# A two-layer attention and expert kernel: a third buffer, earlier clears, and VectorE work given to ScalarE and GpSimd

## The chip, the core and the metric

The kernel runs on one core of a Trainium2 chip. A core has five engines with queues of their own: TensorE (PE; PEld is its weight load) multiplies matrices, VectorE (DVE) works on elements, ScalarE (ACT) applies functions, GpSimd (POOL) works on elements and issues indirect DMAs, and SyncE (SP) issues the other DMAs. Each engine takes its instructions in the order in which they stand in its queue, and semaphores hold an instruction until what it needs is there. The metric is device time in microseconds, the median of several runs.

## The reference

The input x has 8 batches of 112 rows and 256 columns, the context 8 batches of 375 rows and 256 columns. All is in float32. `_layernorm` normalises over the columns, with 1e-5 added to the variance.

```python
x = x + xattn0(layernorm(x), ctx)          # 16 heads of 16, biases, softmax over 375 keys
x = x + moe(layernorm(x))                  # 8 experts, 2 per row, hidden 1024, exact gelu
x = x + xattn1(layernorm(x), ctx, mask)    # no biases; softmax((q k + mask) / 16)
x = x + bitffn(layernorm(x))               # ternary weights, depthwise conv over 3 rows, silu
```

In `moe`, a row is projected into a ball (x Wp + bp, scaled to a norm of at most 0.95), its hyperbolic distance to 8 centroids gives the logits, the two nearest experts are taken, and their outputs are weighted by a softmax of the two. In `bitffn`, both weight matrices (w1 is 1024 x 256, w2 is 256 x 1024) are first made ternary: `s = 1 / clip(mean(abs(w)), 1e-5)`, `clip(round(w * s), -1, 1) / s`.

## The kernel before

**Stages.** Layer 0's attention runs from 0 to about 302 us of the profiled span, with the router of the expert layer woven into it; the experts run to about 465, layer 1's attention to about 681, the ternary feed-forward part to the end.

**One attention batch.** The 16 heads are four groups of four, and the four heads of a group sit at partitions 0, 32, 64 and 96 of TensorE. For batch b the steps are: `norm` (the layer norm is applied, L224 to L226, and n is turned to nT), `query` (t_q, then qd = scaled t_q on VectorE, L560 in layer 0 and L564 in layer 1, then eight DMAs that spread the heads over the partitions, `apart`), `key` (t_k, kd on ScalarE, eight or more DMAs by `apart`), `value` (t_v, copied to v by VectorE, L589 or L593), and for each group g `scores` (sc, and the negated maximum of each row into top, L605 in layer 0; with the mask, L612, in layer 1), once `lower` (the maxima are turned and added to q, giving qa, L625), for each group `turned` (t_p = keys times qa, so that the softmax's exponent comes out with keys on partitions; in layer 1 VectorE adds the mask in four pieces of 336 elements, L645; ScalarE takes Exp into pT, L647) and `weighted` (po = pT times v, L657), and then `finish_o`, `finish_t` and `project` (division by the sum, turn, output product, addition to x at L691 and the next norm's statistics).

**Order.** Both layers run through a plan (L699 to L767), a list of (slot, place, step) that is sorted by slot and place, four slots for each batch. With n = 4b: norm at n-5, key n-4, query n-3, value n-2, scores n+g, lower n+4, turned n+5+g, weighted n+6+g, finish_o n+10, finish_t n+11, project n+12. In layer 0, routing steps 0 to 7 of batch b come at slots n+13 to n+20: step 0 is `Router.norm` (rn, L291 to L294), step 6 is `place` (L371 to L393), which scatters the rows rn to the two places of the row in the DRAM array tok, by two indirect DMAs of GpSimd (L386). The plan of layer 0 has also: `clear` (L187 to L191), which writes zeros over one eighth of tok (slots 4 to 11) or ysc (slots 14 to 21), 0.9 MB each, by DMAs of SP; and the steps that make the weights ternary (L449 to L476, slots 8 to 19): for each of two weights of 2048 elements a partition, two sums of absolute values on VectorE (L457), a product with ones, a small sum and a reciprocal (L465 on), and three element steps. The order on SP is that of the plan; on the other engines a scheduler orders the instructions by their dependences and estimated costs, with the plan as priority.

**Layer norm.** `ln_stats` (L213 to L222) takes mean and variance on VectorE (L216, L218), adds 1e-5 (L219), and calls `rsqrt` (L193 to L211): two integer operations make a first guess, and three Newton steps refine it; for one column that is nine instructions on VectorE, all of one element a partition. The kernel has 32 such norms.

**Layer 1's start.** `combine` (L516 to L528) gathers each row's two expert outputs from ysc with indirect DMAs of GpSimd (L523), and adds them to x on VectorE (L527).

**Buffers.** The pool `ap` has 2 buffers for each name, `ap3` 3, `ap6` 6. rn comes from `ap`. The PSUM pairs are three, shared by t_k, t_v, sc and t_p. The small products of the router and the ternary sums share a bank with po.

```python
for slot, place, step, args in sorted(plan, key=lambda s: s[:2]):
    step(*args)
```

Of the kernel before, what the change touches and what calls it, by code (L numbers as in the profile page):

```python
# [12 lines left out]
F32 = mybir.dt.float32  # L13
# [3 lines left out]
ALU = mybir.AluOpType  # L17
# [37 lines left out]
def xattn_ffn_kernel(  # L55
# [17 lines left out]
    def const(shape, name, dt=F32):  # L73
        return cp.tile(shape, dt, tag=name, name=name)
# [89 lines left out]
    vbuf = [kp.tile([KC, NKC, H, 2 * A], F32, tag="v", name="v") for _ in range(3)]  # L164
    for v in vbuf:
        nc.gpsimd.memset(v, 1.0)
    desc = const([128, E], "desc")
    first = const([128, E], "first")
    for e in range(E):
# [43 lines left out]
    def ln_stats(b):  # L213

        st = sp.tile([S, 6], F32, tag="bnst", name="bnst")
        nc.vector.bn_stats(st, xs[b])  # L216
        mv = sp.tile([S, 2], F32, tag=f"mv{b}", name="mv")
        nc.vector.bn_aggr(mv, st)  # L218
        nc.vector.tensor_scalar_add(mv[:, 1:2], mv[:, 1:2], 1e-5)  # L219
        rs = sp.tile([S, 1], F32, tag=f"rs{b}", name="rs")  # L220
        rsqrt(mv[:, 1:2], rs, 1, "ln")
        return mv, rs  # L222

    def ln_apply(dst, b, stats):  # L224
        mv, rs = stats
        nc.vector.tensor_scalar(dst, xs[b], mv[:, 0:1], rs, ALU.subtract, ALU.mult)  # L226


    kv = [[None] * B, [None] * B]
# [27 lines left out]
    class Router:  # L257
# [30 lines left out]
            nc.vector.tensor_scalar_min(self.cn, self.cn, 0.99)  # L288
            nc.vector.tensor_scalar(self.cn1, self.cn, -1.0, 1.0, ALU.mult, ALU.add)

        def norm(self, b, stats):  # L291
            n = self.pool.tile([S, D], F32, tag="r_n", name="rn")
            ln_apply(n, b, stats)
            return n  # L294

# [152 lines left out]
    def ternary(small):  # L448

        steps = []  # L450
        for i in range(2):
            raw, half = raws[i], F * D // 256
            part, sc = const([128, 16], f"part{i}"), const([128, 1], f"sc{i}")

            def sums(i=i, raw=raw, part=part):
                for h in range(2):
                    yield lambda h=h: nc.vector.tensor_reduce(  # L457
                        part[:, 8 * h : 8 * h + 8],
                        raw[:, h * half : (h + 1) * half].rearrange("p (g n) -> p g n", g=8),
                        AX.X, ALU.add, apply_absolute_value=True,  # L460
                    )

            def scale(i=i, part=part, sc=sc):
                t = small("t_w")
                nc.tensor.matmul(t, ones, part, start=True, stop=True)  # L465
                nc.vector.tensor_reduce(tmean[i], t, AX.X, ALU.add)
# [3 lines left out]
            steps += [  # L470
                *sums(), scale,
                lambda raw=raw, sc=sc: nc.vector.tensor_scalar(raw, raw, sc, 1.0, ALU.mult, ALU.min),
                lambda raw=raw: nc.vector.tensor_scalar(raw, raw, -1.0, MAGIC, ALU.max, ALU.add),
                lambda i=i, raw=raw: nc.vector.tensor_scalar_sub(tern[i], raw, MAGIC),
            ]
        return steps  # L476
# [15 lines left out]
    def attention(layer, stats, stats_next):  # L492
        scale = (0.25, 0.0625)[layer]
        res = None
        with (
# [33 lines left out]

            def norm(b):  # L530
                n = ap.tile([S, D], F32, tag="n", name="n")
                ln_apply(n, b, stats.pop(b))
                if layer == 0:
                    nc.gpsimd.tensor_add(xs[b], xs[b], rowt[:S, D : 2 * D])
# [14 lines left out]
            def query(b):  # L549
                nT = st[b].pop("nT")  # L550
                t = misc("t_q")[:, : 2 * S].rearrange("p (o s) -> p o s", o=2)
                for o in range(2):
                    for c in range(2):
                        nc.tensor.matmul(  # L554
                            t[:, o, :], wts[layer]["q"][:, c, o * 128 : (o + 1) * 128], nT[:, c, :],
                            start=(c == 0), stop=(c == 1),
                        )
# [23 lines left out]
            def value(lay, b):  # L581
                v = kv[lay][b][1]
                t = pair("t_v").rearrange("p i n -> p (i n)")
                for i in range(NKC):
                    value_products(lay, b, i, t[:KC, i * D : (i + 1) * D])
                tv = t[:KC, : NKC * D].rearrange("p (i h a) -> p i h a", i=NKC, a=A)
                if lay == 0:
                    for i in range(NKC):
                        nc.vector.tensor_tensor(  # L589
                            v[:, i, :, 0:A], tv[:, i], rowt[:KC, 0:D].rearrange("p (h a) -> p h a", a=A), ALU.add  # L590
                        )
                else:
                    nc.vector.tensor_copy(v[:, :, :, 0:A], tv)  # L593

            def scores(b, g):

# [31 lines left out]
            def turned(b, g):  # L628
# [11 lines left out]
                for m in range(2):  # L640
                    pT = ap6.tile([KC, 2, NKC * S], F32, tag="pT", name="pT")
                    src = ts[m][:KC, :, : NKC * S]
                    if layer == 1:
                        for i in range(2):
                            nc.vector.tensor_tensor(pT[:, i, :], src[:, i, :], maskT_t, ALU.add)  # L645
                        src = pT
                    nc.scalar.activation(pT, src, AF.Exp)  # L647
                    pTs.append(pT)
# [48 lines left out]
            def add(slot, place, step, *args):  # L697
                plan.append((slot, place, step, args))
# [20 lines left out]
            if layer == 0:  # L719
# [335 lines left out]
```

## Time and profile before

| | |
|---|---|
| median of 3 runs | 786.43 us (785.28 to 789.81) |
| the profiled execution | 775.37 us, its span 773.7 us |
| TensorE busy | 624.8 us, 81% |
| VectorE busy | 462.2 us, 60% |
| ScalarE busy | 225.0 us, 29% |
| GpSimd busy | 48.9 us, 6% |
| mean granted TensorE clock | 0.832 |

The page cuts the span into 40 slices of 19.3 us; a digit is the busy share of a slice in tenths, and PEclk is the clock that TensorE was granted, in tenths.

```profile
PE   5778998969988953999999994999999988744143
DVE  6754769657665484011111105967998897589975
PEclk9787997878977875999999997559999998856557
DMA  3368468731201011697889943101111000000001
```

The experts are the block of nines in the PE row, with VectorE at 0 and 1. In the two attention stages both engines are high, and the clock falls where the PE row falls. The DMA row is high from the fourth to the eighth slice of layer 0, where the clears, the contexts and the first expert weights are loaded. The DMA issues that matter (count, KB each, median time from issue to landing):

```profile
tok<-zero SPq DMA_DIRECT2D x8, 896.0 KB, 5.2
ysc<-zero SPq DMA_DIRECT2D x8, 896.0 KB, 4.4
```

In a timeline a row is an instruction, or several of one kind, with start and length in microseconds; the brackets hold the idle time before it on its engine and the instruction that ended it.

### The profile page before, as it was taken

The page shows a single profiled execution, that of the slowest core. Times are in us where ns is not written, and L with a number is a line of the kernel's source. Part 1 is how long each engine was busy: PE and PEld are TensorE (multiplying, and loading weights), DVE is VectorE, ACT ScalarE, POOL GpSimd, SP SyncE. Part 2 cuts the span into 40 slices and gives each one's busy share as a digit, 9 for nine tenths or more (in the row PEclk, how much of TensorE's full clock was granted, in tenths as well). Part 3 has the DMA queues.
Part 4 walks back from the last instruction along what each step waited for, and adds up shares of the span by engine and source line. Part 5 has one row for each costly group of instructions (what it writes and reads, how often), then busy time and mean ns, then how long its engine had stood idle before and what let it go on. Part 6 is the DMA issues. An engine that isn't in the chain of part 4 may idle for free.

```text
span 773.7 us, 15030 instructions
## 1 busy us (share of the span) xinstructions
PE 624.8 (81%) x5650; PEld 450.1 (58%) x5650; DVE 462.2 (60%) x1663; ACT 225.0 (29%) x452; POOL 48.9 (6%) x89
## 2 busy tenths in 40 slices
PE   5778998969988953999999994999999988744143
PEld 3345665646655642999999983566665655521032
DVE  6754769657665484011111105967998897589975
ACT  1021342313333211433343430123333333317300
POOL 7000000000000010000000006100000000000000
PEclk9787997878977875999999997559999998856557
DMA  3368468731201011697889943101111000000001
GB/s 125 92 200 264 123 188 288 255 108 38 75 2 33 13 52 53 246 325 274 350 316 359 355 167 95 40 7 28 27 24 24 18 20 2 1 1 0 0 12 36
DMA packets 45269, 89.70 MB, mean 116 GB/s; under 512 B 7324, under 2 KB 36364, under 8 KB 39820
## 3 DMA queue, kind: packets, MB, share of 16 engines
q1 hardware_dynamic: 42028, 83.33, 32.5%
q0 software_dynamic: 1536, 3.67, 1.6%
q10 hardware_dynamic: 1632, 1.72, 0.7%
q8 instruction: 45, 0.74, 0.4%
q14 instruction: 28, 0.23, 0.1%
HBM read 60.54 MB, written 20.19 MB: 104 GB/s over the span
## 4 chain that ended last, share of the span: by engine, by line
PE 62%; DVE 20%; DMA 7%; issue 4%; ACT 2%; SPq 2%; POOL 0%; DVEq 0%; ACTq 0%; POOLq 0%
PE t_h L827 10%; PE t_y L838 9%; PE sc L602 8%; PE t_p L635 7%; PE po L657 5%; PE t_v L247 5%; PE t_k L240 4%; DMA tok<-rn,at 2%; DVE top L605 2%; PE t_q L554 2%; SPq L547 2%; DVE am L952 2%; PE t_out L690 2%; PE t_o L669 1%; DMA we<-in_WA_dram 1%
## 5 line engine op out<-in xcount | busy, mean ns | idle before, releaser
L602 PE MATMUL sc<-k,q 32*112 32x375 f32 x512 | 99.3, 613 | 12.2 <-DMA k<-kd 6.0
L827 PE MATMUL t_h<-tnT,we 128*128 128x128 f32 x672 | 92.4, 282 | 0.2
L827 PEld LDWEIGHTS t_h<-tnT,we 128*128 128x128 f32 x672 | 88.0, 195 | 7.3 <-ACT hT L831 1.9
L831 ACT ACTIVATE hT<-t_h,we 128x128 f32<-128x128 f32 x168 | 61.3, 368 | 91.8 <-PE t_h L827 86.3
L635 PE MATMUL t_p<-qa,k 32*125 32x112 f32 x1536 | 81.1, 314 | 7.3 <-DVE top L605 4.2
L838 PE MATMUL t_y<-we,hT 128*128 128x256 f32 x336 | 82.8, 380 | 0.0
L635 PEld LDWEIGHTS t_p<-qa,k 32*125 32x125 f32 x1536 | 64.0, 207 | 26.2 <-issue 15.5
L647 ACT ACTIVATE pT<-t_p 125x672 f32<-125x672 f32 x64 | 43.3, 728 | 111.4 <-PE t_p L635 111.4
L647 ACT ACTIVATE pT<-pT 125x672 f32<-125x672 f32 x64 | 48.8, 763 | 92.1 <-DVE pT L645 89.9
L605 DVE TENSOR_REDUCE top<-sc 112x2 f32<-112x750 f32 x64 | 57.9, 934 | 24.0 <-PE sc L602 23.8
L657 PE MATMUL po<-pT,v 125*32 125x112 f32 x1536 | 63.9, 287 | 8.8 <-ACT pT L647 5.9
L645 DVE TENSOR_TENSOR pT<-t_p,maskT 125x336 f32<-125x336 f32 x128 | 56.7, 501 | 17.4 <-PE t_p L635 16.8
L612 DVE CUSTOM_DVE_ANT_0 sm<-sc,mask 112x375 f32<-112x375 f32 x128 | 62.8, 543 | 0.6 <-PE sc L602 0.6
L838 PEld LDWEIGHTS t_y<-we,hT 128*128 128x128 f32 x336 | 59.1, 191 | 5.5
L657 PEld LDWEIGHTS po<-pT,v 125*32 125x32 f32 x1536 | 41.8, 119 | 34.3 <-ACT pT L647 17.3
L602 PEld LDWEIGHTS sc<-k,q 32*112 32x112 f32 x512 | 34.4, 201 | 43.1 <-issue 16.9
L240 PE MATMUL t_k<-ctx,wk 128*128 128x375 f32 x128 | 53.0, 560 | 6.8 <-DMA ctx<-in_ctxT_dram 6.1
L816 DVE COPY tnT<-t_tn 128x256 f32<-128x256 f32 x21 | 8.9, 425 | 78.4 <-PE t_tn L814 71.4
L247 PE MATMUL t_v<-wv,ctx 128*125 128x256 f32 x192 | 50.1, 411 | 3.4 <-DVE top L605 3.4
L840 DVE TENSOR_TENSOR y<-t_y,we 128x256 f32<-128x256 f32 x21 | 8.9, 425 | 68.9 <-PE t_y L838 65.4
L247 PEld LDWEIGHTS t_v<-wv,ctx 128*125 128x125 f32 x192 | 37.3, 202 | 11.4 <-DVE top L605 4.1
L240 PEld LDWEIGHTS t_k<-ctx,wk 128*128 128x128 f32 x128 | 26.9, 223 | 26.4 <-issue 14.2
(208 smaller groups left out, 741.4 us busy)
## 6 DMA issues: line engine op xcount, KB each, us to landing
we<-in_WB_dram SPq DMA_DIRECT2D x21, 1152.0 KB, 7.8
we<-in_WA_dram SPq DMA_DIRECT2D x21, 1028.0 KB, 6.0
tok<-zero SPq DMA_DIRECT2D x8, 896.0 KB, 5.2
ysc<-zero SPq DMA_DIRECT2D x8, 896.0 KB, 4.4
k<-kd SPq DMA_DIRECT2D x120, 46.9 KB, 2.1
ctx<-in_ctxT_dram SPq DMA_DIRECT2D x8, 375.0 KB, 4.7
tn<-tok SPq DMA_DIRECT2D x21, 128.0 KB, 7.3
ysc<-y SPq DMA_DIRECT2D x21, 128.0 KB, 3.3
```

Of the source, the lines that this page charges most:

```text
L240: nc.tensor.matmul(t, wts[layer]["k"][:, c, g * 128 : (g + 1) * 128], ctx_t[b][:, c, :], start=(c == 0), stop=(c == 1),)
L247: nc.tensor.matmul(t, ctx_t[b][:, c, i * KC : (i + 1) * KC], wts[layer]["v"][:, c, :], start=(c == 0), stop=(c == 1),)
L602: nc.tensor.matmul(ts[j // 2][:S, j % 2, :SK], q[r, g, :], k[r, g, :], start=True, stop=True)
L605: nc.vector.tensor_reduce(top[:, g, 2 * m : 2 * m + 2, A : A + 1], ts[m][:S, :, :SK], AX.X, ALU.max, negate=True,)
L612: nc.vector.tensor_tensor_reduce(out=sm, in0=ts[m][:S, i, :SK], in1=mask_t, scale=-1.0, scalar=3.0e38, op0=ALU.add, op1=ALU.min, accum_out ...
L635: nc.tensor.matmul(ts[j // 2][:KC, j % 2, c * S : (c + 1) * S], k[r, g, c * KC : (c + 1) * KC], qa[r, g, :], start=True, stop=True,)
L645: nc.vector.tensor_tensor(pT[:, i, :], src[:, i, :], maskT_t, ALU.add)
L647: nc.scalar.activation(pT, src, AF.Exp)
L657: nc.tensor.matmul(po[32 * j : 32 * j + 32, g, :], v[:, c, 4 * g + j, :], pTs[j // 2][:, j % 2, c * S : (c + 1) * S], start=(c == 0), stop ...
L827: nc.tensor.matmul(ph[:, i, :], w1[:, c, f * 128 : (f + 1) * 128], nt[:, c, :], start=(c == 0), stop=(c == 1),)
L831: nc.scalar.activation(hT[:, f, :], ph[:, i, :], AF.Gelu, bias=b1[:, f : f + 1])
L838: nc.tensor.matmul(py, hT[:, f, :], w2[:, f, :], start=(f == 0), stop=(f == NF - 1))
```

## The change

Six edits. A third buffer holds the routed rows: rn is taken from `ap3`. The clears of tok and ysc go two to a slot, tok at slots 4 to 7 and ysc at 8 to 11. The sums of absolute values are one ScalarE instruction for each weight, whose elementwise output goes to the tile that later holds the ternary weight; the ternary steps are ten in place of twelve. The root of a layer norm is an addition and a power of -0.5 on GpSimd. In layer 1, qd and v are made by ScalarE, and n by GpSimd from the second batch on. The mask of layer 1 is added for the first two heads of a group by one VectorE instruction of 672 elements, and for the other two by ScalarE, which copies t_p to SBUF, and GpSimd, which adds the mask there.

```diff
+    minus_half = const([128, 1], "mhalf")
+    nc.gpsimd.memset(minus_half, -0.5)
...
         nc.vector.bn_aggr(mv, st)
-        nc.vector.tensor_scalar_add(mv[:, 1:2], mv[:, 1:2], 1e-5)
         rs = sp.tile([S, 1], F32, tag=f"rs{b}", name="rs")
-        rsqrt(mv[:, 1:2], rs, 1, "ln")
+        nc.gpsimd.tensor_scalar_add(rs, mv[:, 1:2], 1e-5)
+        nc.gpsimd.tensor_tensor(rs, rs, minus_half[:S], ALU.pow)
         return mv, rs
...
-    def ln_apply(dst, b, stats):
+    def ln_apply(dst, b, stats, eng=None):
         mv, rs = stats
-        nc.vector.tensor_scalar(dst, xs[b], mv[:, 0:1], rs, ALU.subtract, ALU.mult)
+        (eng or nc.vector).tensor_scalar(dst, xs[b], mv[:, 0:1], rs, ALU.subtract, ALU.mult)
...
-        def norm(self, b, stats):
-            n = self.pool.tile([S, D], F32, tag="r_n", name="rn")
+        def norm(self, b, stats, pool):
+            n = pool.tile([S, D], F32, tag="r_n", name="rn")
...
             def sums(i=i, raw=raw, part=part):
-                for h in range(2):
-                    yield lambda h=h: nc.vector.tensor_reduce(
-                        part[:, 8 * h : 8 * h + 8],
-                        raw[:, h * half : (h + 1) * half].rearrange("p (g n) -> p g n", g=8),
-                        AX.X, ALU.add, apply_absolute_value=True,
-                    )
+
+                nc.scalar.activation(tern[i], raw, AF.Abs, accum_out=part)

             def scale(i=i, part=part, sc=sc):
-                t = small("t_w")
+                t = small("t_w")[:, 0:1]
                 nc.tensor.matmul(t, ones, part, start=True, stop=True)
-                nc.vector.tensor_reduce(tmean[i], t, AX.X, ALU.add)
-                nc.vector.tensor_scalar(tmean[i], tmean[i], 1.0 / (F * D), 1e-5, ALU.mult, ALU.max)
+                nc.vector.tensor_scalar(tmean[i], t, 1.0 / (F * D), 1e-5, ALU.mult, ALU.max)
                 nc.vector.reciprocal(sc, tmean[i])
...
             def norm(b):
                 n = ap.tile([S, D], F32, tag="n", name="n")
-                ln_apply(n, b, stats.pop(b))
+                ln_apply(n, b, stats.pop(b), nc.gpsimd if layer == 1 and b > 0 else nc.vector)
...
-                    nc.vector.tensor_scalar_mul(qd, t, scale)
+                    nc.scalar.mul(qd, t, scale)
...
-                    nc.vector.tensor_copy(v[:, :, :, 0:A], tv)
+                    nc.scalar.copy(v[:, :, :, 0:A], tv)
...
                     if layer == 1:
-                        for i in range(2):
-                            nc.vector.tensor_tensor(pT[:, i, :], src[:, i, :], maskT_t, ALU.add)
+
+                        eng = nc.vector
+                        if m == 1:
+                            nc.scalar.copy(pT, src)
+                            eng, src = nc.gpsimd, pT
+                        eng.tensor_tensor(
+                            pT, src, maskT_t.unsqueeze(1).to_broadcast([KC, 2, NKC * S]), ALU.add
+                        )
                         src = pT
                     nc.scalar.activation(pT, src, AF.Exp)
...
-                        r["n"] = rt.norm(b, stats_next.pop(b))
+                        r["n"] = rt.norm(b, stats_next.pop(b), ap3)
...
                 for e in range(E):
-                    add(4 + e, 8, clear, tok, e)
-                    add(14 + e, 8, clear, ysc, e)
+                    add(4 + e // 2, 8, clear, tok, e)
+                    add(8 + e // 2, 8, clear, ysc, e)
```

More of the change, by code (lines that the diff above doesn't have):

```diff
@@ L451, in ternary @@
         for i in range(2):
-            raw, half = raws[i], F * D // 256
-            part, sc = const([128, 16], f"part{i}"), const([128, 1], f"sc{i}")
+            raw = raws[i]
+            part, sc = const([128, 1], f"part{i}"), const([128, 1], f"sc{i}")
             def sums(i=i, raw=raw, part=part):
-                for h in range(2):
-                    yield lambda h=h: nc.vector.tensor_reduce(
-                        part[:, 8 * h : 8 * h + 8],
-                        raw[:, h * half : (h + 1) * half].rearrange("p (g n) -> p g n", g=8),
-                        AX.X, ALU.add, apply_absolute_value=True,
-                    )
+                nc.scalar.activation(tern[i], raw, AF.Abs, accum_out=part)
             def scale(i=i, part=part, sc=sc):
-                t = small("t_w")
+                t = small("t_w")[:, 0:1]
                 nc.tensor.matmul(t, ones, part, start=True, stop=True)
-                nc.vector.tensor_reduce(tmean[i], t, AX.X, ALU.add)
-                nc.vector.tensor_scalar(tmean[i], tmean[i], 1.0 / (F * D), 1e-5, ALU.mult, ALU.max)
+                nc.vector.tensor_scalar(tmean[i], t, 1.0 / (F * D), 1e-5, ALU.mult, ALU.max)
                 nc.vector.reciprocal(sc, tmean[i])
             steps += [
-                *sums(), scale,
+                sums, scale,
                 lambda raw=raw, sc=sc: nc.vector.tensor_scalar(raw, raw, sc, 1.0, ALU.mult, ALU.min),
```

## The prediction, made before the changed kernel ran

> **What bounds the kernel now.** I read the busy rows first, then busy time by stretches of 20 us, then TensorE's timeline for the idle time in front of its instructions, then the chain of waits through the longest of these, and last the groups of the operations that the change touches.
>
> ```profile
> PE 624.8 (81%) x5650; PEld 450.1 (58%) x5650; DVE 462.2 (60%) x1663; ACT 225.0 (29%) x452; POOL 48.9 (6%) x89
> ...
> PE 62%; DVE 20%; DMA 7%; issue 4%; ACT 2%; SPq 2%; POOL 0%; DVEq 0%; ACTq 0%; POOLq 0%
> ```
>
> TensorE leads, VectorE holds the next part of the chain; ScalarE and GpSimd have room. In the stretches (columns: stretch, length, busy time of PE, PEld, DVE, ACT, POOL with counts, granted clock, DMA share, GB/s) the stages differ:
>
> ```profile
> 120.00:140.00 20.00, 16.64 (x155) 11.93 (x155) 16.73 (x77) 4.70 (x9) 0.72 (x1) 0.74 0.76 259
> 160.00:180.00 20.00, 16.82 (x182) 12.23 (x182) 12.62 (x46) 5.88 (x13) 0.72 (x1) 0.74 0.33 106
> 480.00:500.00 20.00, 18.57 (x72) 10.12 (x72) 18.56 (x93) 2.32 (x4) 5.78 (x7) 0.50 0.19 54
> 560.00:580.00 20.00, 19.49 (x259) 12.77 (x256) 19.50 (x79) 6.87 (x11) 0.00 (x0) 1.00 0.11 24
> ```
>
> In layer 0 (0 to 302 us) TensorE is interrupted and then granted 0.74 of its clock; early layer 1 runs at 0.50; in steady layer 1 TensorE and VectorE are both full. The mixture of experts (302 to 465) is TensorE's alone and the feed-forward part (681 to 774) mostly VectorE's; the change touches neither beyond the norms.
>
> TensorE's timeline at its stalls (start, us, then in brackets the idle time before and its releaser):
>
> ```profile
> 58.69 5.48 PE L247 MATMUL t_v<-wv,ctx 128*125 128x256 f32 x12 [3.37 <-DVE top L605]
> ...
> 73.87 0.91 PE L635 MATMUL t_p<-qa,k 32*125 32x112 f32 x20 [2.56 <-DVE top L605]
> ...
> 125.52 0.76 PE L657 MATMUL po<-pT,v 125*32 125x112 f32 x20 [2.57 <-DVE w1mean L466]
> ...
> 162.56 0.77 PE L554 MATMUL t_q<-nT,wq 128*128 128x112 f32 x2 [7.15 <-DVE qa L625]
> ```
>
> Each ends on VectorE. The first two stand behind the absolute sums (L457), the third behind two layer norms and a routing step, the fourth behind a layer norm's output that waits for a DMA:
>
> ```profile
> 143.31 10.67 DMA we<-in_WA_dram
> 153.98 4.45 DMA tok<-rn,at
> 158.43 0.03 issue
> 158.48 0.05 issue
> 158.53 0.41 DVE rn L226
> ```
>
> The chain says: rn (two buffers) waits for the scatter that reads its old contents, and that scatter had waited in the DMA queues behind three clears and a weight load.
>
> **What the Trainium skill says.** "TensorE: Matmul & The Clock Gate", Part 1: the clock drops to half after an idle window of about 3.4 us. The trace agrees: after the 7.15 us stall a t_q of 8 matmuls took 2.05 us against 1.15 at 192.31, and the clock came back at about 170. "SBUF — State Buffer", Who interferes with whom: GpSimd shares a port pair, an exclusive lock, with VectorE instructions in a two-port mode or with two SBUF inputs. The trace has candidates (a GpSimd add from 10.49 to 11.22 covers a 0.73 us L207, mean 0.225), so GpSimd's new work can lengthen VectorE's. "GPSIMD Engine Reference", 3.1, and "ScalarE: Activation LUTs", What ACT_TABLE_LOAD costs, give the two prices used below. No page prices a power on GpSimd.
>
> **The change part by part.** Sums are against the profiled execution (775.4 us, span 773.7); the median of the runs, 786.4, is 1.4% longer, and I scale by that at the end.
>
> *Sums on ScalarE (two ternary weights).* Removed from VectorE: 4 x 1.212 us (L457) and two small reduces. Added: two passes over 2048 elements; the ScalarE page's price, 280 ns + 0.833 ns each, gives an estimate of 2.0 us. They lie in ScalarE's idle time (29% busy), but kd, pT and nT queue behind them, and the first can wait 2.5 us there for its weight's DMA, as L457 did. Gone: 3.37 and 2.56 us of stall and the slow matmuls after each (t_v 5.48 against 2.8, t_k 4.48 against 2.79), together 10.3 us.
>
> *Clears moved.* 16 clears of 0.896 MB go through SP's queue by slot 11 instead of slot 21. Between the q DMAs of batch 2 and the k DMAs of batch 4 lie now six clears of ysc (5.4 MB) where three of tok and a WA (3.7 MB) lay. At about 345 GB/s, the rate of the busy stretches, that is +5 us for k(4), and q(4) follows it; k(2), q(2), k(3) and q(3) are passed by earlier clears as well. WA and WB loads come later, but are used only at 302. So most of the 10.3 us that TensorE comes forward is spent waiting for k(4): I take 2 of it as kept at 115 us (bounds -8 and +4), including +1.5 for the start, where GpSimd's powers stand between its 1.43 us k copies and batch 0's norm.
>
> *Third rn buffer, and clears out of the way at 140.* The 7.15 us stall and the half clock after it (about 3.4 us) go: -10.5. The rn now waits one batch further back. The smaller stalls of the same kind (1.16 + 1.16 at 215, 0.98 + 1.62 at 240, each with a slow stretch after it) shrink: -6 (bounds 0, -10).
>
> *Roots on GpSimd.* Per norm VectorE loses L219 0.149, L201 0.150, L202 0.209, L204 0.207 and 3 x (0.225 + 0.157) = 1.86 us; 32 norms, 60 us of VectorE. GpSimd gets an add and a power on [112,1]; the trace shows no power. From below 0.09 us (a memset of [128,1], 88 ns), from above 2 us each; I take 0.4 for the power and 0.1 for the add. At 123 us this clears two norms (3.7 us) from the backlog before w1mean: stall 2.57 and the half clock to 136 (4.4) go, -7. At layer 0's tail -2. What is late next: in GpSimd's queue the second scatter of a pair waits for the first to land (about 2.5 us), and a norm behind it waits too; six batches at 1 us, +6 (bounds 0 and +12).
>
> Layer 0: -2 - 10.5 - 6 - 7 - 2 + 6 = -21.5.
>
> *Layer 1.* A batch takes 21.95 us (period from 544.66 to 610.54, three batches); its matmuls at full clock sum to 18.8. VectorE loses per batch: masks, 16 x 0.501 less 4 adds over 672 elements (estimate 0.97 each, a little under two of 0.501) = 4.1; v copy 0.957; qd 0.389; n 0.410; two norms 3.7; 9.5 of some 20.
>
> ```profile
> L645 DVE TENSOR_TENSOR pT<-t_p,maskT 125x336 f32<-125x336 f32 x128 | 56.7, 501 | 17.4 <-PE t_p L635 16.8
> L647 ACT ACTIVATE pT<-pT 125x672 f32<-125x672 f32 x64 | 48.8, 763 | 92.1 <-DVE pT L645 89.9
> L534 POOL TENSOR_TENSOR x<-x,rows 112x256 f32<-112x256 f32 x8 | 5.8, 722 | 110.8 <-DVE n L226 76.3 <-DVE f L361 23.8 <-DVE rs L202 10.7
> ```
>
> ScalarE gets per group a copy of 672 elements (0.73, as the Exp that reads PSUM). GpSimd's add over 672: the trace has 0.722 us for 256; the GpSimd page's 4497 ns at 2048 gives a slope of 2.1 ns, so 1.6 us (estimate; below 1.2 by the page's best case, above 3.8 if the port lock holds it through VectorE's work). ScalarE runs copy, Exp, then Exp behind the add and cannot pass it: 0.73 + 1.8 + 0.76 = 3.3 per group, 13.2 per batch, plus kd 0.78, v 0.96, qd, nT, oT 0.35 each, ou 0.53: 16.5 of a period of 19 to 22. So ScalarE isn't the bound, but is near it; kd and v, queued behind the second Exp, hold PSUM pairs up to 1.8 us longer. I remove the stall seen only in group 0 (sc 1.69 at 591.67 against 0.90, behind a norm's ten instructions) and some of the rest: -1.3 for six batches, -8; the ramp at half clock, VectorE 18.56 of 20, -2; the start +1.5, because the first norm's power stands behind ten gathers (0.96 us each from 467.7, so to 479; VectorE's n was at 479.2). Together -8.5. Feed-forward: 0.
>
> **Sum.** -30: 745.4 profiled, x 786.4/775.4 = 756, and I take 757.
>
> **Rivals.**
> *The clears cost more than they free.* k(4) comes late enough to eat all 10.3 (+2 in place of -2), and the first scatters still find full queues, so that half of the rn stalls stays (-5 for -10.5, -3 for -6). For: a DMA share of 0.76 from 120 to 140; against: the clears also end earlier. Layer 0 is then 2 - 5 - 3 - 7 - 2 + 6 = -9, layer 1 -6: 760 profiled, 771.
> *Everything goes.* The early gain is kept (-8 for -2), GpSimd's queue delays no norm (0 for +6), and layer 1 runs at 19.6 us a batch (six times 2.35 = -14, with ramp and start -14.5): -33.5 - 14.5 = -48, 727 profiled, 738. For: TensorE's pure 18.8; against: scores still wait for the PSUM pair that the add over t_p frees.
> *Slower: ScalarE and GpSimd become layer 1's bound.* With d from the copy's end to the second Exp, ScalarE needs 4 x (1.49 + d) + 3.3 a batch; it passes 21.95 at d = 3.2, and eats layer 0's whole gain of 21.5 at 2.7 us a batch more, d = 3.85. The add must take some 3.7 us, 2.3 times my estimate: the lock, or broadcast masks read slowly. At d = 4.2, 8 x 4.1 = +33 - 21.5 = +11.5: 787 profiled, 798. For: both SBUF operands and VectorE half busy; against: the nearest row.
>
> **How the numbers follow.** Forecast 0.44 (745 to 768), late clears 0.25 (768 to 783), all goes 0.20 (728 to 745), slower 0.11. The range 735 to 781 leaves out about 2 in 10: the slower case, a third of the best one and the worst of the late clears. About 0.5%, 4 us, is what a measurement of this kernel can tell from nothing. Faster: 0.44 + 0.20 + 0.20 of the late clears = 0.84; the rest of those, 0.05, is no difference; slower 0.11.
>
> **What would show it.** Right: no TensorE idle above 2 us at 55 to 75, no rn waiting for a scatter, TensorE's clock 1.0 at 125 to 170, VectorE under 13 of 20 in steady layer 1 with a period of 20 to 21. Wrong: k(4)'s DMAs much later than 105 with TensorE idle before sc; a power above 1 us; the second Exp waiting over 3 us for GpSimd; t_v or t_k waiting for ScalarE's copies.

## The result, and the profile after

The changed kernel is 1.3% slower: 793.5 us median (786.4 to 801.3, 20 runs) against 783.8 us (777.3 to 789.8, 20 runs), ratio 1.0129, 95% interval 1.010 to 1.0157. The forecast was 757 in a range of 735 to 781.

The busy rows and the shares of the chain, from the page of the changed kernel:

```profile
PE 635.2 (80%) x5650; PEld 457.7 (58%) x5650; DVE 387.0 (49%) x1218; ACT 259.2 (33%) x504; POOL 135.9 (17%) x193
...
PE 56%; DVE 17%; POOL 8%; DMA 6%; issue 6%; ACT 5%; SPq 2%; DVEq 0%; POOLq 0%; ACTq 0%
```

The work moved as planned: VectorE has 387 us where it had 462, with 445 instructions fewer. But GpSimd, which had no share in the chain that ended last, now has 8%, and ScalarE 5% where it had 2%. One engine was unloaded, and the two that took its work came onto the path.

The groups of the new work (columns: count, then busy time and mean ns of one, then the idle time of the engine before them and what ended it):

```profile
L646 POOL TENSOR_TENSOR pT<-pT,maskT 125x672 f32<-125x672 f32 x32 | 51.6, 1611 | 114.4 <-ACT pT L644 114.4
L223 POOL TENSOR_TENSOR rs<-rs,mhalf 112x1 f32<-112x1 f32 x32 | 18.4, 574 | 2.3
L228 POOL TENSOR_SCALAR n<-x,mv,rs 112x256 f32<-112x256 f32 x7 | 8.9, 1272 | 5.1 <-PE t_n L534 4.5
L222 POOL TENSOR_SCALAR rs<-mv 112x1 f32<-112x1 f32 x32 | 7.6, 236 | 124.8 <-DVE mv L220 120.5 <-DVE r L213 4.1
L650 ACT ACTIVATE pT<-pT 125x672 f32<-125x672 f32 x64 | 48.7, 763 | 34.7 <-POOL pT L646 30.5
L646 DVE TENSOR_TENSOR pT<-t_p,maskT 125x672 f32<-125x672 f32 x32 | 27.5, 858 | 49.1 <-PE t_p L632 49.1
```

The prices of the large instructions were near the estimates: the GpSimd addition took 1.61 us (estimate 1.6), and VectorE's joined addition, one of 672 elements in place of two of 336, took 0.86 (0.97). A root took 0.24 + 0.57 us, where 0.1 + 0.4 had been assumed. What the page adds is the waiting: ScalarE stood 30.5 us before its second Exp, waiting for GpSimd's addition.

The stretch of steady layer 1 (columns as before) that stood at 19.49 for PE and 19.50 for DVE:

```profile
560.00:580.00 20.00, 18.10 (x238) 11.47 (x236) 12.05 (x39) 10.26 (x16) 6.69 (x5) 1.00 0.13 26
```

VectorE has 12.05 of 20, ScalarE 10.26, GpSimd 6.69: none of these three is full, and TensorE, at 18.10, does less than before. That points to a latency, not to a busy engine.

By stages, from TensorE's timelines, in us. Layer 0 lasts to the first t_h and the experts to the end of the last t_y; then come the time to the t_out of layer 1's first batch, four further batches, the last three, and the rest. A period below is the time from one batch's t_out to the next one's.

| profiled execution of | layer 0 | experts | first batch | next four | last three | rest |
|---|---|---|---|---|---|---|
| before | 305.8 | 158.7 | 77.5 | 87.8 | 49.2 | 94.7 |
| after | 311.0 | 158.1 | 85.6 | 91.3 | 55.4 | 94.3 |
| after, a later execution | 308.7 | 160.1 | 86.4 | 91.3 | 52.3 | 94.3 |

The profiled execution of before (775.4 us) is shorter than all its 20 timed runs, and that of after (797.6) is above its median, so the table shows 22 us where the medians show 10. Both attention layers lost; experts and feed-forward part stayed. The same layer-1 code of the kernel before took 49.2 us for the last three batches at a granted clock of 0.86 and 53.9 us at 0.70 (in the run with the third buffer alone), so differences of 5 us in that column are not read. Nor are those of the first batch, which took 76.1 to 80.7 us with that same code.

Layer 1's loss in the chain of waits of the changed kernel (start, us, engine, what):

```profile
557.52 0.57 POOL rs L223
558.09 0.19 POOL rs L222
...
558.36 0.57 POOL rs L223
558.93 0.10 issue
559.03 1.24 POOL n L228
560.27 1.59 POOL pT L646
561.86 0.02 issue
561.88 0.77 ACT pT L650
562.66 0.04 issue
562.70 0.77 PE po L660 x20
```

Two roots, n and the mask addition stand in GpSimd's queue one behind the other; Exp waits for the last, and TensorE's po for Exp. In the kernel before, the chain at this place holds TensorE's instructions alone:

```profile
554.13 0.58 PE t_o L669 x4
554.71 0.94 PE po L657 x24
555.65 0.85 PE t_p L635 x24
```

Taken from start to start in TensorE's timeline, all po of the second period take 3.1 us in the kernel before and 5.7 in the changed kernel; all sc take 5.8 and 4.7. So VectorE's relief does show, in sc, and the waits before po outweigh it.

Layer 0's loss shows in SP's timeline, with the keys of batch 3 on ScalarE beside it. First the kernel before:

```profile
67.36 1.34 SPq L130 DMA_DIRECT2D mask<-in_mask_dram  x1
...
80.30 5.31 SPq L547 DMA_DIRECT2D k<-kd  x8
...
87.23 5.76 SPq L547 DMA_DIRECT2D q<-qd  x8
```

```profile
79.23 1.04 ACT L576 ACTIVATE kd<-t_k,cols 128x375 f32<-128x375 f32 x2 [3.15 <-PE t_k L240]
```

Then the changed kernel:

```profile
70.62 4.24 SPq L190 DMA_DIRECT2D tok<-zero  x4
74.90 4.90 SPq L130 DMA_DIRECT2D mask<-in_mask_dram  x1
...
81.10 3.51 SPq L190 DMA_DIRECT2D tok<-zero  x2
84.74 7.44 SPq L544 DMA_DIRECT2D k<-kd  x8
92.23 1.28 SPq L190 DMA_DIRECT2D ysc<-zero  x2
93.61 7.32 SPq L544 DMA_DIRECT2D q<-qd  x8
```

```profile
77.78 1.04 ACT L573 ACTIVATE kd<-t_k,cols 128x375 f32<-128x375 f32 x2 [2.80 <-PE t_k L242]
```

In the kernel before, SP has nothing to issue from 72.1 us on, and the k DMAs of batch 3 start as soon as kd is there (80.27). In the changed kernel kd is there earlier, at 78.82, but SP is still issuing clears and mask loads: the first mask load behind the clears holds SP for 4.90 us in place of 1.34. The k DMAs start 5.9 us late, and the q DMAs of batch 3 stand behind them and behind two more clears, and start at 93.61 in place of 87.23. From there to the first scores of batch 3 it takes 6.0 us (99.62) against 5.9 before (93.16): the delay of 6.4 us is there before the first q DMA is issued, and not in its transfer. Two other kernels with early clears, b_early_clears and best1_early below, show the same: the mask load takes 3.39 and 4.86 us, and q of batch 3 starts at 92.26 and 93.32.

### The profile page after: what moved, and what is told of

Its sections match the earlier page's. It is cut to its first block, busy times and chain, and to the rows that moved or that the text cites. A ratio compares the mean times of both kernels' runs of the same rounds, so it can differ in the third digit from the quotient of the medians.

```text
span 795.7 us, 14684 instructions
## 1 busy us (share of the span) xinstructions
PE 635.2 (80%) x5650; PEld 457.7 (58%) x5650; DVE 387.0 (49%) x1218; ACT 259.2 (33%) x504; POOL 135.9 (17%) x193
## 4 chain that ended last, share of the span: by engine, by line
PE 56%; DVE 17%; POOL 8%; DMA 6%; issue 6%; ACT 5%; SPq 2%; DVEq 0%; POOLq 0%; ACTq 0%
PE t_h L830 10%; PE t_y L841 9%; PE t_p L632 7%; PE sc L599 6%; PE po L660 6%; PE t_v L249 5%; POOL pT L646 3%; PE t_k L242 3%; ACT pT L650 2%; DMA q<-qd 2%; DVE top L602 2%; DVE am L955 2%; PE t_y L973 1%; PE t_out L693 1%; DVE y L944 1%
## 5 line engine op out<-in xcount | busy, mean ns | idle before, releaser
L599 PE MATMUL sc<-k,q 32*112 32x375 f32 x512 | 95.3, 608 | 10.5 <-DMA q<-qd 3.6
L632 PE MATMUL t_p<-qa,k 32*125 32x112 f32 x1536 | 87.3, 335 | 6.4 <-DVE qa L622 3.4
L830 PEld LDWEIGHTS t_h<-tnT,we 128*128 128x128 f32 x672 | 87.8, 194 | 7.2 <-ACT hT L834 1.9
L834 ACT ACTIVATE hT<-t_h,we 128x128 f32<-128x128 f32 x168 | 61.4, 368 | 91.1 <-PE t_h L830 85.6
L632 PEld LDWEIGHTS t_p<-qa,k 32*125 32x125 f32 x1536 | 70.1, 227 | 25.8 <-issue 15.8
L660 PE MATMUL po<-pT,v 125*32 125x112 f32 x1536 | 72.6, 299 | 15.4 <-ACT pT L650 15.2
L609 DVE CUSTOM_DVE_ANT_0 sm<-sc,mask 112x375 f32<-112x375 f32 x128 | 62.8, 543 | 20.8 <-PE sc L599 20.1
L660 PEld LDWEIGHTS po<-pT,v 125*32 125x32 f32 x1536 | 45.7, 123 | 46.0 <-ACT pT L650 26.2
L646 POOL TENSOR_TENSOR pT<-pT,maskT 125x672 f32<-125x672 f32 x32 | 51.6, 1611 | 114.4 <-ACT pT L644 114.4
L650 ACT ACTIVATE pT<-pT 125x672 f32<-125x672 f32 x64 | 48.7, 763 | 34.7 <-POOL pT L646 30.5
L646 DVE TENSOR_TENSOR pT<-t_p,maskT 125x672 f32<-125x672 f32 x32 | 27.5, 858 | 49.1 <-PE t_p L632 49.1
L520 POOL DMA_INDIRECT yg<-ysc,at x16 | 15.5, 966 | 170.7 <-issue 170.2
```

The lines of the kernel that those rows point to most:

```text
L599: nc.tensor.matmul(ts[j // 2][:S, j % 2, :SK], q[r, g, :], k[r, g, :], start=True, stop=True)
L609: nc.vector.tensor_tensor_reduce(out=sm, in0=ts[m][:S, i, :SK], in1=mask_t, scale=-1.0, scalar=3.0e38, op0=ALU.add, op1=ALU.min, accum_out ...
L632: nc.tensor.matmul(ts[j // 2][:KC, j % 2, c * S : (c + 1) * S], k[r, g, c * KC : (c + 1) * KC], qa[r, g, :], start=True, stop=True,)
L646: eng.tensor_tensor(pT, src, maskT_t.unsqueeze(1).to_broadcast([KC, 2, NKC * S]), ALU.add)
L660: nc.tensor.matmul(po[32 * j : 32 * j + 32, g, :], v[:, c, 4 * g + j, :], pTs[j // 2][:, j % 2, c * S : (c + 1) * S], start=(c == 0), stop ...
L830: nc.tensor.matmul(ph[:, i, :], w1[:, c, f * 128 : (f + 1) * 128], nt[:, c, :], start=(c == 0), stop=(c == 1),)
```

## The experiments

Each is read as a ratio to the kernel before with its 95% interval, and by the stages of its profile. Differences between two ratios are given in per cent of the kernel before. From one chip to the next a ratio of the same kernel moved by up to 0.4% (the changed kernel 1.0129 and 1.0167, best1 0.957 and 0.9563); of the six variants of best1, the first four ran on another chip than best1, and the last two on the same chip as a repeat of best1.

**The clears back in their old slots.**

```diff
-                    add(4 + e // 2, 8, clear, tok, e)
-                    add(8 + e // 2, 8, clear, ysc, e)
+                    add(4 + e, 8, clear, tok, e)
+                    add(14 + e, 8, clear, ysc, e)
```

> The changed kernel with the clears back at slots 4 to 11 (tok) and 14 to 21 (ysc). Theory (the early clears stand in the DMA queues ahead of the q DMAs of batches 2 and 3 and hold TensorE): scores of batch 3 come at 93 us or earlier in place of 99.6, layer 0 ends 7 to 10 us earlier than in the changed kernel, ratio to the kernel before about 1.002. Rival (layer 0 loses by GpSimd's roots and ScalarE's long sums, and the clears only hide it): the first 120 us stay within 3 us of the changed kernel, ratio 1.010 or more.

Measured: 1.0139 (1.0096 to 1.0183), no gain. The first 120 us follow the theory: q of batch 3 starts at 84.69 us, and t_out of batch 1 comes at 114.96 in place of 126.70. Layer 0 ends at 305.0, 4 to 6 us earlier than in the changed kernel's two profiles. Between them a stall of 5.33 us before t_q at 160.03 took much of the gain back. GpSimd's timeline shows where it starts:

```profile
144.35 1.19 POOL L388 DMA_INDIRECT tok<-rn,at  x1 [22.20 <-DVE at L386]
150.65 0.94 POOL L388 DMA_INDIRECT tok<-rn,at  x1 [5.11 <-DMA tok<-rn,at]
151.61 0.26 POOL L222 TENSOR_SCALAR rs<-mv 112x1 f32<-112x1 f32 x1
```

The second scatter waits 5.11 us for the first to land, and the root of the next norm stands behind it in GpSimd's queue. So the earlier clears cost in one place and, with the roots on GpSimd, spare in another. Why the ratio shows nothing of the remaining 4 to 6 us stays open.

**All of the mask on VectorE.**

```diff
-                        if m == 1:
-                            nc.scalar.copy(pT, src)
-                            eng, src = nc.gpsimd, pT
```

> The changed kernel with all mask additions of layer 1 on VectorE, each one instruction of 672 elements (0.86 us in the trace); ScalarE's copy and GpSimd's addition gone. Theory (the chain copy, add, Exp of 3.1 us holds po and ScalarE): the period of a layer-1 batch falls from 22 to 23.7 to below 21.5, layer 1 is 10 to 15 us shorter, ratio about 0.997. Rival (layer 1 loses by the roots and n on GpSimd): period falls by less than 0.7, ratio 1.006 to 1.010. Rival (VectorE becomes the bound again): ratio 1.013 or more.

Measured: 0.9864 (0.9815 to 0.9913), a larger gain than expected. The period of a batch is 20.8 us where the changed kernel had 23.3, 23.7, 22.2 and 22.0; first batch 75.4, next four 83.2, last three 48.6. In the profiles layer 1 is thus 23 to 25 us shorter than in the changed kernel, and 7 us shorter than in the kernel before. Taking out one part of the change turns a loss of 1.3% into a gain of 1.4%. VectorE, with 15.8 of 20 us busy, is not the bound.

**The roots as Newton steps on VectorE.**

```diff
-        nc.gpsimd.tensor_scalar_add(rs, mv[:, 1:2], 1e-5)
-        nc.gpsimd.tensor_tensor(rs, rs, minus_half[:S], ALU.pow)
+        nc.vector.tensor_scalar_add(mv[:, 1:2], mv[:, 1:2], 1e-5)
+        rsqrt(mv[:, 1:2], rs, 1, "ln")
```

> The changed kernel with the layer norms' roots as Newton steps on VectorE. Theory (GpSimd's queue is what delays: 0.24 + 0.57 us a root, and roots stand before the mask additions): layer 1's first two periods fall from 23.5 to 22, its start comes 2 us earlier, ratio 1.006. Rival (VectorE's backlog returns): layer 0 is 5 us longer or more, ratio 1.015 or more.

Measured: 1.0104 (1.0064 to 1.0144), between the two forecasts, and not to be told from the changed kernel's 1.0129. Layer 0 ends at 304.2, some 5 to 7 us earlier. Whether the first periods fall is not shown: this profile's clock was 0.91 from 560 to 620 us, where the changed kernel had 1.00. By itself, with the mask's chain still there, the run decides nothing.

**The third buffer alone, in the kernel before.** Its diff is the two lines of `Router.norm` and its call.

> The kernel before with the third buffer for rn alone. Theory (the 7.15 us stall at 155 to 162 and the half clock after it go): layer 0 ends 7 to 10 us earlier, ratio 0.988 to 0.991. Rival (what was behind that stall, VectorE's backlog and the k DMAs, ends it a little later anyway): 0 to 4 us, ratio 0.995 to 1.000.

Measured: 0.9831 (0.9786 to 0.9875), 13 us, more than the expectation above; layer 0 ends at 289.0, 16.8 us earlier. The stall of 7.15 us is 1.43 at 156.00, and nothing took its place. This part did what the prediction said.

**The mask's split alone, in the kernel before.** The diff is that of the change in `turned`.

> The kernel before with the split of the mask alone: half on VectorE in one instruction, half by ScalarE's copy and GpSimd's addition; roots, n, qd and v as before, so that GpSimd's queue holds nothing but the additions. Theory (the chain copy, add, Exp of 3.1 us is late for po by itself): the period of a layer-1 batch is 22.5 to 23.5, ratio 1.01 to 1.02. Rival (it is the two roots and n ahead of the addition in GpSimd's queue, 2.8 us once a batch, that make it late): the period falls to 21.5 or less, ratio 0.995 or less.

Measured: 1.0155 (1.0072 to 1.0237), from four runs. Steady periods rose only from 22.0 to 22.3: in the second of them sc takes 4.7 us from start to start in place of 5.8, and po 4.2 in place of 3.1, so VectorE's relief and the longer chain nearly balance. The last three batches took 54.7 us at a clock of 0.71; as the old code took 53.9 at 0.70, nothing can be read from that, and where most of the 1.5% lies stays open. The chain of this kernel, with nothing but the additions and the old work of GpSimd in its queue:

```profile
553.70 0.73 ACT pT L646
554.43 0.07 issue
554.50 1.62 POOL pT L648
556.12 0.02 issue
556.14 0.77 ACT pT L652
556.91 0.04 issue
556.96 0.77 PE po L662 x20
```

From t_p to po it is 3.3 us over three engines. TensorE fills most of this with other work and then waits 0.61 us for the Exp, once a batch.

**The earlier clears alone, in the kernel before.**

> The kernel before with the earlier clears alone. Theory (they hold the q DMAs of batches 2 and 3): scores of batch 3 come 5 to 9 us later than at 93; of that the scatter stall at 155 (rn waiting behind clears of ysc, 7.15 us) gives back as much, as no clear is left there: ratio 0.995 to 1.005. Rival (the delay stays in full and the stall stays too): 1.008 or more. Rival (the clears were only in the way at 140): 0.985 to 0.990, as the third buffer alone.

Measured: 1.0071 (1.0042 to 1.010), above what was expected. t_out of batch 1 comes 12.2 us later (128.15), layer 0 ends 6.0 us later: the stall at 155 went, and half of the delay was given back.

**The roots on GpSimd alone, in the kernel before.**

> The kernel before with the layer norms' roots on GpSimd alone. Theory (a root of 0.24 + 0.57 us and its two hand-overs stop VectorE, whose next instruction waits for it, and stands behind the scatter that waits for the one before): layer 0 ends 0 to 8 us later, ratio 1.000 to 1.010. Rival (the 1.86 us that VectorE is spared are worth their stalls, as the prediction counted): layer 0 ends 5 us earlier or more, ratio 0.990 or less.

Measured: 1.0028 (0.9979 to 1.0077), no difference that can be measured; layer 0 ends 3 us later. VectorE loses 320 instructions whose mean durations add up to 60 us, but its busy time falls by 33 us only (462.2 to 429.2), a first sign that these durations overlap others. Nothing comes of it.

**The change without what had shown no gain (best1).** The changed kernel with late clears, the mask on VectorE, n on VectorE, and GpSimd's roots only for the norms after layer 1's attention. The third buffer, the sums, and qd and v on ScalarE stay. Part of the diff:

```diff
-        nc.gpsimd.tensor_scalar_add(rs, mv[:, 1:2], 1e-5)
-        nc.gpsimd.tensor_tensor(rs, rs, minus_half[:S], ALU.pow)
+        if on_pool:
+            nc.gpsimd.tensor_scalar_add(rs, mv[:, 1:2], 1e-5)
+            nc.gpsimd.tensor_tensor(rs, rs, minus_half[:S], ALU.pow)
+        else:
+            nc.vector.tensor_scalar_add(mv[:, 1:2], mv[:, 1:2], 1e-5)
+            rsqrt(mv[:, 1:2], rs, 1, "ln")
...
-                stats_next[b] = ln_stats(b)
+                stats_next[b] = ln_stats(b, layer == 1)
```

> The changed kernel with the clears in their old slots, all mask additions on VectorE in one instruction for each half, n on VectorE, and GpSimd's roots for the norms after layer 1's attention alone. Theory: layer 0 ends as with the third buffer alone, near 295 us, a batch of layer 1 takes 20.8 us, ratio 0.965 to 0.978. Rival (what VectorE takes back makes it the bound again): period 21.5 or more, ratio 0.983 or more, no better than the third buffer alone.

Measured: 0.957 (0.9511 to 0.9629), 742.9 us median, better than forecast and better than both kernels. Its stretch of steady layer 1:

```profile
560.00:580.00 20.00, 19.60 (x250) 12.73 (x250) 15.49 (x45) 9.27 (x14) 0.79 (x2) 1.00 0.13 27
```

TensorE is at 19.60, with VectorE at 15.49: less spread out than in the changed kernel, and faster. Layer 0 ends at 285.0 (283.5 in a later profile), and a batch takes 20.8 to 21.2 us. The next six runs change one part of it each.

**best1 with the earlier clears.**

> The version best1 with the earlier clears. Theory (the clears hold the q DMAs of batches 2 and 3, and in the changed kernel this was made up for by the scatter no longer standing behind clears in front of the roots): with the roots on VectorE the cost is bare: scores of batch 3 come 6 to 10 us later, layer 0 ends 7 to 12 us later, ratio 0.966 to 0.973. Rival (the clears cost nothing, as the run with late clears said): ratio 0.952 to 0.962.

Measured: 0.9723 (0.9643 to 0.9803); layer 0 ends 17.5 us later, all of it there by t_out of batch 1 (129.33 against 111.61). So the clears cost 1.5% here; in the run with late clears, the root that waits for a scatter hid much of that.

**best1 with every root on GpSimd.**

> The version best1 with every root on GpSimd. Theory (a root queues behind the second scatter of a pair, which waits for the first to land while clears of ysc fill the queues): TensorE has a stall of 4 us or more near 155 as in the run with late clears, layer 0 ends 6 to 10 us later and layer 1 starts 1 to 4 us later after the experts, ratio 0.966 to 0.975. Rival (the stall at 160 of the run with late clears came from the late DMAs of the keys): ratio 0.955 to 0.962.

Measured: 0.9897 (0.9862 to 0.9932), 3.3% above best1, more than expected. Layer 0 ends 16.1 us later. The stall near 155 is there but with 2.96 us (at 159.49) smaller than expected, and one of 4.50 us at 130.31, where best1 has 3.06 (at 122.19), comes before any scatter has been issued. In VectorE's timeline there:

```profile
123.11 0.42 DVE L228 TENSOR_SCALAR rn<-x,mv,rs 112x256 f32<-112x256 f32 x1
123.44 0.16 DVE L352 SCALAR_TENSOR_TENSOR dif<-dif,den 112x8 f32<-112x8 f32 x1
124.29 0.41 DVE L228 TENSOR_SCALAR n<-x,mv,rs 112x256 f32<-112x256 f32 x1 [0.69 <-POOL rs L223]
```

VectorE stands still until the root comes back, with the routing's next steps, which don't need it, queued behind n. In layer 0 it stands so 14 times, 11.2 us in all. For the stretch around that row best1 needs fewer microseconds with more instructions: from the addition to x to qa it is 7.2 us (114.33 to 121.51), here 8.6 (121.01 to 129.63). Rows of best1's VectorE timeline show how:

```profile
118.17 0.21 DVE L209 SCALAR_TENSOR_TENSOR a<-rs,h 112x1 f32<-112x1 f32 x1
118.30 0.22 DVE L366 SCALAR_TENSOR_TENSOR oh<-v,m,desc 112x8 f32<-112x8 f32 x1
118.43 0.15 DVE L213 SCALAR_TENSOR_TENSOR rs<-a,rs 112x1 f32<-112x1 f32 x1
118.55 0.16 DVE L367 TENSOR_REDUCE f<-oh 112x1 f32<-112x8 f32 x1
```

A step of the root (L209, L213) and one of the routing (L366, L367) alternate, each starting 0.12 to 0.13 us after the one before, although each lasts 0.15 to 0.22: in these rows an instruction starts before the one ahead has ended, where it doesn't need its result. With the root away, the routing's steps, each of which needs the one before, follow each other at 0.19 to 0.27 us (125.57, 125.77, 126.03, 126.22, 126.49 in best1_roots). The root lay in gaps that the routing leaves. This accounts for a part of the 16.1 us: t_out of batch 0 is already 6.7 us later (95.99 against 89.31; 91.25 in best1's later profile), and of that no more is shown than the first four waits for a root, 4.4 us of VectorE.

**best1 with the sums of absolute values on VectorE.**

> The version best1 with the sums of absolute values on VectorE as in the kernel before. As the prediction had it, the stalls at 58 and 73 return and cost up to 10 us: ratio 0.965 to 0.970. Rival (the q and k DMAs of batches 2 to 4 bound the first 100 us, so that the stalls are hidden): layer 0 ends within 3 us, ratio 0.955 to 0.961.

Measured: 0.9659 (0.9598 to 0.972), 7 us above best1, at intervals that overlap a little and on another chip. The stalls at 58 and 73 are back (4.93 us at 60.70 and 2.56 at 75.36); layer 0 ends 6.5 us later. This part gains, somewhat less than the 10.3 us that its stalls came to.

**best1 with two additions of 336 elements.**

> The version best1 with the mask added in two instructions of 336 elements for each half, 2 x 0.50 in place of 0.86 us. Theory (a PSUM pair comes free 0.14 us later in each of eight additions, and VectorE has 1.1 us more a batch, in a period that TensorE's waits for the pair partly set): period 21.0 to 21.4 in place of 20.8, ratio 0.957 to 0.962. Rival (period unchanged, as VectorE has 4 of 20 us to spare): ratio 0.952 to 0.957. If the period goes back to 22, the joined addition was what shortened layer 1.

Measured: 0.977 (0.9717 to 0.9824), 2.0% above best1, more than either expected; periods of 21.1 and 21.8. The profile gives 1.7 us for the four steady batches; 5 us of layer 0, whose code is the same, and 7 of the last three batches (49.2 at a clock of 0.74; best1_sums, with best1's layer 1, took 48.5 at 0.72) are of the size that moves between executions. That joining the additions helps is seen in the periods; how much, the two readings leave open.

**best1 with each VectorE root computed twice.**

```diff
             rsqrt(mv[:, 1:2], rs, 1, "ln")
+            r2 = sp.tile([S, 1], F32, tag="r2", name="r2")
+            rsqrt(mv[:, 1:2], r2, 1, "l2")
```

> The version best1 with each VectorE root computed a second time, from the same variance into a tile that nothing reads, 24 norms of nine more instructions. As the prediction counted (mean durations add up): 1.7 us a norm, layer 0 ends 10 us later or more, ratio 0.975 or more. Theory (VectorE starts an instruction that depends on nothing running after some 0.07 us, so that a root lies in the gaps of the routing chain): layer 0 ends less than 6 us later, ratio 0.957 to 0.966.

Measured: 0.9706 (0.965 to 0.9763), against 0.9563 (0.95 to 0.9625) of best1 on the same chip; layer 0 ends 5.4 us later, and the profiled spans differ by 5.1. The ratio lies between the two forecasts, the layer within the theory's. The ratios differ by 11 us, with 5 to 18 allowed by their intervals. The 216 instructions have mean durations near 0.19 us (nine make 1.7 us), 41 us in all; VectorE's busy time grew by 14 us (434.3 to 448.2). So an eighth of such time by the profiles, a quarter by the medians, is on the path: not all of it and not none. As nothing waits for the second root, the run prices the engine's time, and not the time for which the first root keeps n waiting.

**best1 with the mask's split put back.**

> The version best1 with the split of the mask put back (ScalarE's copy, GpSimd's addition for half). GpSimd's queue holds two roots before an addition once a batch, and no n. Theory (the chain exposes po, most where no keys and values are left to compute): period 22 or more in place of 20.8, layer 1 12 to 22 us longer, ratio 0.972 to 0.985. Rival (the loss needs GpSimd's n and all roots ahead of the additions): less than 6 us, ratio 0.964 or less.

Measured: 0.9843 (0.9794 to 0.9893), 2.8% or 22 us above best1 on the same chip. Periods of 22.2; first batch 83.0 against 77.3, next four 88.7 against 84.1, last three 53.3 against 41.9. The clock in the last three was 0.75 against 0.94, and best1_sums, with best1's layer 1, took 48.5 there at 0.72, so that more than half of this last difference may be the clock. TensorE's wait before po, in the third of these periods:

```profile
584.16 0.77 PE L664 MATMUL po<-pT,v 125*32 125x112 f32 x20 [0.60 <-ACT pT L654]
```

In the same period of best1 this wait is not there. No n and no root of layer 1's start stands in GpSimd's queue here, so the split costs its time by itself.

**best1 and the changed kernel on the same chip as the last two.**

> The version best1 once more, on the same chip as the other three, so that they can be set against it: ratio 0.953 to 0.963.

> The changed kernel on the same chip as the other three: ratio 1.010 to 1.016.

Measured: 0.9563 (0.95 to 0.9625) and 1.0167 (1.0111 to 1.0222), the second just above what was expected.

## Why the prediction was wrong

*The mask's split* is the step that failed most. The prediction priced the addition rightly: 1.6 us, worked out from the trace's 0.722 us at 256 elements and the 4497 ns at 2048 that the GPSIMD Engine Reference of the Trainium skill gives in section 3.1; 1.611 was measured. It then asked only whether ScalarE has room: "So ScalarE isn't the bound". It has room, 10.26 of 20 us. But TensorE's po waits for the end of copy, addition and Exp, 3.3 us, against 0.86 + 0.76 with VectorE's addition, and TensorE has only about 2.7 us of other work in between: it waits 0.61 us before po once a batch with the split alone, and 1.14 + 0.62 in the changed kernel's second period, where GpSimd has roots and n ahead of the addition. In place of "Together -8.5" layer 1 is 16 to 18 us longer in the profiles, and with the split taken out it is 7 us shorter than in the kernel before. The rival on the slower side had the place, but not the mechanism: by throughput it began to decide at d = 3.2 us between copy and Exp, and with the split alone the loss was there at d = 1.7 (554.43 to 556.14 us). That roots and n add to the split is read from the chain and from the first periods (23.3 and 23.7 against 22.2); no run takes n alone away.

The prediction also feared that GpSimd's work lengthens VectorE's instructions. In the large ones this isn't seen: a masked score took 543 ns before and after, a row maximum 934, and the joined addition 858 with GpSimd's additions beside it against 852 without (a_mask_dve).

*Roots on GpSimd.* Two terms failed. "At 123 us this clears two norms (3.7 us) from the backlog" added mean durations as if VectorE worked one instruction after the other; the Newton steps overlapped the routing chain, and the doubled root shows between an eighth and a quarter of its durations on the path. And the wait that the change adds, VectorE's for GpSimd, was costed only behind scatters ("six batches at 1 us"); it stops VectorE at n and rn also where no scatter is near, mostly for 0.65 to 0.73 us, with the routing behind. Alone the roots were worth nothing (1.0028), in the changed kernel they made no clear difference, and with the other stalls gone they cost 3.3%. That the waits are the whole of this is not shown: they come to 11.2 us of VectorE in layer 0, which ends 16.1 us later.

*Clears.* The direction was right, the place and size were not. The prediction looked for the loss at the keys of batch 4 and kept 2 us of gain at 115. Its six clears against three are those behind the q DMAs of batch 3; from the q DMAs of batch 2 on, which it named, there are fourteen against seven. The wait that it left out is that of k and q of batch 3 in SP's queue, which is held up by the issuing of the clears and mask loads; t_out of batch 1 came 10.8 us later. The rival of late clears came nearest here. The cost is 0.7% alone and 1.5% in best1.

*Third buffer.* Right, and the clears had no part in it: -10.5 and -6 were forecast for it and the moved clears together, and 16.8 us in layer 0 were measured for the buffer alone.

*Sums on ScalarE.* Half right: 7 us of 10.3 in best1. The sum waits on ScalarE for its weight's DMA, an Exp stands behind it, and TensorE behind that:

```profile
58.29 1.91 ACT L459 ACTIVATE w0q<-we 128x2048 bf16<-128x2048 f32 x1 [6.32 <-DMA we<-in_w1T_dram]
```

```profile
60.96 1.51 PE L599 MATMUL sc<-k,q 32*112 32x375 f32 x8 [2.77 <-ACT pT L650]
```

So a stall of 2.77 us took the place of the 3.37 that was to go. In the changed kernel nothing of the gain is left: the first scores of batch 2 wait for q's DMAs and come at 70.37 us against 70.22.

*Layer 1's start.* As forecast in size: t_q comes 17.8 us after the experts' end against 16.2 (+1.6). Whether GpSimd's powers are the reason stays open, for two runs with the first roots on VectorE also show 18.0 (b_third_buffer and best1_split).

Set against each other, the third buffer (-1.7%), the sums (-0.9%) and VectorE's relief in layer 1 were outweighed by split (+1.5 to +2.8%), roots (up to +3.3%) and clears (+0.7 to +1.5%). The parts don't add exactly, since a stall of one hides that of another: roots and late clears together show it. The least settled numbers are the joined addition's and the roots' in the changed kernel; what qd and v on ScalarE do by themselves no run tells.

## What to carry to other kernels

Work moved off a busy engine is paid for in hand-overs: before moving it, write down the chain from the producer to the consumer that waits, and set its new length against what that consumer has to do meanwhile. Whether the new engine has room is another question. Small dependent steps on one engine may cost a fraction of their durations when another chain interleaves with them, so that removing them gains little, and a wait put in their place can cost more than they did. Large transfers of no urgency are placed by what small urgent transfers stand behind them in the same queue; there the time in which the queue issues them counts, and not only the bytes.

## What the hardware showed that was not expected

- On GpSimd a subtraction and multiplication with two per-partition operands over 112 x 256 (n) took 1.27 us, against 0.72 us for the addition of two tiles of that size on the same engine, and 0.41 us for the same n on VectorE.
- A power of one element a partition took 0.57 us on GpSimd and an addition of a constant 0.24 us; in layer 0 of best1_roots VectorE waited for such roots 14 times, 0.8 us on the mean.
- On SP the issuing of a mask load took 1.34 us in the kernel before, behind two clears, and 4.90 in the changed kernel, behind four.
- VectorE's addition from PSUM took 0.501 us for 336 elements a partition and 0.858 for 672, so joining two saves 0.14 us.
